# The branch hints of three engines read a second word of the flag

## The chip, the cores and the metric

The kernel runs on one core of a Trainium2 chip. The time is the device time of one execution in microseconds, given as the median of several runs. The core has five engines with instruction streams of their own: TensorE (PE; its weight loads are shown as PEld), VectorE (DVE), ScalarE (ACT), GpSimd (POOL) and SyncE (SP, which here issues most of the DMAs). An engine's sequencer also executes instructions that occupy no data path: register loads, branches, semaphore waits.

## What is computed

The reference works on x of 8 sequences x 128 tokens x 512 channels in float32 and adds two blocks to it. Cut to what matters:

```
x = x + ffn0(cond0(x))          # cond0: x @ W.T plus a gated low-rank term of two experts in eight
                                # ffn0: 4-bit weights (packed, with zeros and scales by groups), silu(gate) * up, down
x = x + ffn1(cond1(x))          # cond1: x[b] @ weight[id[b]].T, ffn1: rms norm, silu(gate) * up, down
```

In ffn0 a weight is `scale[g_idx[i]] * (q - (zero[g_idx[i]] + 1))`. The kernel has a fast way of handling scales that supposes the usual order of the group indices and scales of ordinary size, and a second, general way for any other input.

## The kernel before

The work is written out twice in one program. `network(..., True, ...)` is the whole computation with ffn0 done by groups of scales (`by_groups_of_scales`); behind it stands a branch, `tc.If(again[0] > 0, ...)` at L1719, and under it `network(..., False)`, the whole computation once more with ffn0 done in float32 (`in_float32`). With the inputs of this case the second one is never executed: each engine jumps over it to the end of the program.

What decides is a flag. `verdict` makes a count, for each of 128 partitions, of the conditions met by indices and scales. In the second block's plan the task "count" adds the counts by one small matmul (`met`, L971) into a PSUM bank, and the task "judge" (`told`, L974) compares the sum with the number wanted on VectorE and writes 1 into the flag if it is smaller, else 0. The flag is an int32 word in SBUF, with room around it (`FLAG_PLACE`).

The first block is in an order written by hand: ten and a last chunk of 128 inner channels, gate and up products on TensorE over four groups of the contraction and two halves of the tokens, with rescaling of the PSUM sums between groups by ScalarE or VectorE, which also unpack and dequantise the next chunks. The second block is ordered by a planner (`Plan`): every step is a task with an estimated time, its dependencies and a key (a due time), and the tasks are emitted in the order in which the planner's model begins them. The inner dimension has 14 chunks (`chunk`), each with 42 matmuls of 128x512 for gate and up; the weights are split into parts (`w`, `wz`), and the down products (`down`, L1628) run in blocks of two or three chunks. Each engine executes its own stream in that order.

The engines learn the flag in `high_low` (L1641): at the first product of the last down block every engine loads the word into a register (`values_load`), and TensorE, VectorE and ScalarE (the list `FETCHED`) get a branch hint named "again" that takes its value from this register. All of this stands in the engines' streams among matmuls and other work: TensorE's load comes between products of the last gate/up chunk (L1480) and down products (L1628). After the load SyncE also executes two check instructions of the sequencer. The branch itself (L1719) stands behind the last work of each engine, 20 us later. The outputs are written by SyncE, the last piece by ScalarE (L1690, L1692), and behind the branch SyncE waits for all output DMAs before the closing barrier (L1876).

Of the kernel before, what the change touches and what calls it, by code (L numbers as in the profile page):

```python
# [16 lines left out]
I32 = mybir.dt.int32  # L17
# [4 lines left out]
ALU = mybir.AluOpType  # L22

P = 128
# [76 lines left out]
GU_PLACE, FLAG_PLACE, COND_PLACE = 64, 24, 48  # L101
# [6 lines left out]
FETCHED = [EngineType.PE, EngineType.DVE, EngineType.Activation]  # L108
# [11 lines left out]
NGOOD = KC + NJ0 + 3 * (2 * NJ0 + KC)  # L120
# [12 lines left out]
class Plan:  # L133
# [5 lines left out]
    def add(self, name, engines, fn, deps=(), key=0.0, takes=(), gives=()):  # L139
        t = Task(name, engines, fn, deps, key, takes, gives)  # L140
        for d in t.deps:
            d.then.append(t)
        self.tasks.append(t)
        return t
# [77 lines left out]
def network_in(ctx, tc, a, out, by_groups, flag, again):  # L222
    nc = tc.nc
# [371 lines left out]
    def by_groups_of_scales():  # L595
# [375 lines left out]
            nc.tensor.matmul(ps[:1, :1], lhsT=count[0][:, 0:1], rhs=count[0][:, 1:2], start=True, stop=True)  # L971

        def told(ps):
            nc.vector.tensor_scalar(flag[:1], ps[:1, :1], float(NGOOD * P), None, ALU.is_lt)  # L974

        judges.append((met, told))


# [230 lines left out]
    def of(k, *who):  # L1209
        x = plan.place[k, who]  # L1210
        return late_tiles[x] if isinstance(x, tuple) else x

    def pe(us):
        return {"pe": us}
# [4 lines left out]
    def dve(n):  # L1219
        return {"dve": 0.075 + n / 960}  # L1220

    def either(n):
        return act(n) | dve(n)
# [177 lines left out]
    if judges:  # L1401
        judge = judges.pop()
        met = add(
            "count", pe(0.2), lambda _: judge[0](of("bank", "judge")), [normed[ROWS1[0]]], 2 * ROW, [("bank", ("judge",))]
        )
# [170 lines left out]
    def h_tile(j, tb):  # L1576
        x = of("h3", j, tb)
        return x if len(x.shape) == 3 else x.rearrange("p i n k -> p i (n k)")

    def down_weights(j, k):  # L1580
        raw = add(
            "wd", {"sp": 0.4}, lambda _: nc.sync.dma_start(out=of("wd", j), in_=a["wd1"][:, j, :]), [fd_open], k - 10.0,
            [("wd", (j,))],
        )

        def high(_):
            nc.scalar.activation(of("d", j)[:, 0], of("wd", j), AF.Copy, scale=HSCALE)

        def large(_):
            nc.scalar.activation(of("wd", j), of("wd", j), AF.Copy, scale=1.0 / EPS)  # L1590

        def low(_):
            d = of("d", j)
            nc.vector.scalar_tensor_tensor(d[:, 1], d[:, 0].bitcast(F32), -1.0 / EPS, of("wd", j), ALU.mult, ALU.add)

        def diff(_):
            d = of("d", j)
            nc.vector.tensor_tensor(d[:, 2], d[:, 0].bitcast(F32), d[:, 1].bitcast(F32), ALU.subtract)

        t0 = add("d hi", act(D), high, [raw], k, [("d", (j,))])  # L1600
        t1 = add("d large", act(D), large, [t0], k)
        t2 = add("d lo", dve(D), low, [t1], k, (), [("wd", (j,))])
        t3 = add("d di", dve(D), diff, [t2], k)
        d_ready[j] = (t0, t2, t3)

    def down(j0, j1):
        k, n = begin["down", j0], j1 - j0
        last = j1 == NJ1
        for j in range(j0, j1):
            down_weights(j, k - DOWN_LEAD + D_STEP * (j - j0))  # L1610
        users = []
        parts = [(tb, m, 0, TB) for tb in range(NTB) for m in range(KC)]
        if last:
            tb, m = parts.pop()[:2]
            parts += [(tb, m, c0, c0 + TB // 2) for c0 in (0, TB // 2)]
        for i, (tb, m, c0, c1) in enumerate(parts):
            kk = k + 3 * n * PASS * i
            who = ("down", j0, m, tb, c0)
            mine, t, w = [], None, c1 - c0
            one = PASS * w / TB + (0.007 if w < TB else 0.0)  # L1620

            d_first = last and i >= NTB * KC - 1
            first_key = k + 3 * n * PASS * (NTB * KC - 1) - D_FIRST
            firsts = (2, j0) if d_first else (0, j0)

            def products(j, which, m=m, tb=tb, who=who, c0=c0, c1=c1, firsts=firsts):
                for i in which:
                    nc.tensor.matmul(  # L1628
                        of("bank", *who)[:, : c1 - c0],
                        lhsT=of("d", j)[:, i, m * P : (m + 1) * P],  # L1630
                        rhs=h_tile(j, tb)[:, i, c0:c1],
                        start=((i, j) == firsts),
                        stop=True,
                        skip_group_check=(i, j) != firsts,
                    )

            def sums(t, key, takes=()):
                for j in range(j0, j1):
                    def high_low(_, j=j, products=products, tell=(last and i == 0 and j == j0)):
                        if tell and by_groups:  # L1640
                            again.append(nc.values_load(flag[:1, :], min_val=0, max_val=1))  # L1641
                            tc.mark_branch_hint_location("again", hint=again[0], engines=FETCHED)
                        products(j, (0, 1))

                    t = add(
                        "down H", pe(2 * one), high_low, [*h_ready[j, tb][:2], *d_ready[j][:2], t], key,
                        takes if j == j0 else (),
                    )
                    mine.append((j, t))
                return t  # L1650

            def differences(t, key, some, takes=()):
                def fn(_, products=products):
                    for j in some:
                        products(j, (2,))

                needs = [x[2] for j in some for x in (h_ready[j, tb], d_ready[j])]
                t = add("down D", pe(len(some) * one), fn, [t, *needs], key, takes)
                mine.extend((j, t) for j in some)
                return t  # L1660

            def rescaled(t, by, key):
                def fn(e, who=who, w=w):
                    ps = of("bank", *who)[:, :w]
                    scaled(e, ps, ps, by)

                return add("rescale", either(w), fn, [t], key)

            takes = [("bank", who)]
            if d_first:  # L1670
                t = None
                for j in range(j0, j1):
                    t = differences(t, first_key, [j], takes if j == j0 else ())
                t = rescaled(t, DSCALE, first_key)
                t = sums(t, kk)
            else:
                t = sums(None, kk, takes)
                t = rescaled(t, HLSCALE, kk + R_AT)
                t = differences(t, kk + (DD_LAST if last and i == NTB * KC - 2 else DD_AT), range(j0, j1))
            by_end = 1.0 + EPS if d_first else -EPS  # L1680

            def done(_, i=i, m=m, who=who, by_end=by_end, cols=slice(tb * TB + c0, tb * TB + c1)):
                x = xT[:, m, cols]
                ps = of("bank", *who)[:, : cols.stop - cols.start]
                nc.vector.scalar_tensor_tensor(x, ps, by_end, x, ALU.mult, ALU.add)  # L1685
                if last:
                    by = nc.scalar if i == NTB * KC - 1 else nc.sync
                    if i == 1:
                        some = out[: 2 * P, cols].rearrange("(m p) t -> p m t", p=P)
                        by.dma_start(out=some, in_=xT[:, :2, cols])  # L1690
                    elif i > 1:
                        by.dma_start(out=out[m * P : (m + 1) * P, cols], in_=x)  # L1692

            add("done", dve(w), done, [t], kk + DONE_AT, (), [("bank", who)])
            users += [(j, tb, t) for j, t in mine]
        for j in range(j0, j1):
            for tb in range(NTB):
                add("h3", {None: 0.0}, None, [t for jj, tt, t in users if (jj, tt) == (j, tb)], k, (), [("h3", (j, tb))])
            add("d", {None: 0.0}, None, [t for jj, _, t in users if jj == j], k, (), [("d", (j,))])
# [11 lines left out]
@with_exitstack  # L1711
def adaln_ffn_kernel(ctx: ExitStack, tc: tile.TileContext, a, out):
    nc = tc.nc

    outer = ctx.enter_context(tc.tile_pool(name="outer", bufs=1, side="right"))
    flag = outer.tile([P, FLAG_PLACE], I32, name="flag")[:, :1]
    again = []
    network(tc, a, out, True, flag, again)
    with tc.If(again[0] > 0, preferred_fallthrough_block=True, label="again", name="again"):  # L1719
        network(tc, a, out, False)  # L1720
# [160 lines left out]
```

## Time and profile before

| | us |
|---|---|
| median of 3 runs | 413.8 (413.66 to 414.06) |
| the profiled execution | 413.65 |
| its span, first to last instruction | 411.6 |
| busy: TensorE | 405.0 |
| busy: VectorE | 368.2 |
| busy: ScalarE | 304.4 |
| last matmul begins | 406.3 |
| last VectorE instruction ends | 407.1 |
| SyncE sees the last output landed | 409.9 |

The profile is of one execution. Times in it count from the start of the span. Of a group of instructions by line the three durations are shortest, median and longest in ns; an engine name with a q (PEldq, DVEq, SPq) is a sequencer's instruction, during which the data path may go on with what was issued before. The granted TensorE clock was 0.999 over the span. The trace also records DMA packets, among them the fetches of instructions, which come in pieces of 16 KB for TensorE and of 8 KB for other engines.

### The profile page before, as it was taken

How to read it: one execution, taken by the hardware profiler on the slowest of the kernel's cores; microseconds unless marked ns; L12 is line 12 of the kernel's file. 1: busy time of each engine (PE TensorE's matmuls, PEld its weight loads, DVE VectorE, ACT ScalarE, POOL GpSimd, SP SyncE). 2: the span in 40 equal slices, each digit the busy share in tenths (PEclk: the TensorE clock that was granted, in tenths of full speed). 3: DMA queues.
4: the chain of work that ended last, by engine and by line, in shares of the span. 5: the costliest groups of instructions: out<-in, count | busy, mean ns of one | idle time of the engine just before them, and what ended most of it. 6: DMA issues, size and time to landing. Idle time of an engine off the chain costs nothing.

```text
span 411.6 us, 5202 instructions
## 1 busy us (share of the span) xinstructions
PE 405.0 (98%) x1779; PEld 319.3 (78%) x1779; DVE 368.2 (89%) x677; ACT 304.4 (74%) x502; POOL 28.9 (7%) x35
## 2 busy tenths in 40 slices
PE   9999999999999999999999999999999999999995
PEld 9886788888888867445778888888888888888884
DVE  4998989997999788988999999989999899988974
ACT  5943788858896786487999888867976688767751
POOL 1000200000000400421020011011011101000000
PEclk9999999999999999999999999999999999999999
DMA  8930820120020540782153214313423225000005
GB/s 282 398 150 7 254 73 7 46 58 2 0 64 2 197 135 2 257 303 40 51 160 73 64 25 125 100 31 92 110 57 91 73 45 135 4 2 1 25 2 209
DMA packets 17041, 38.59 MB, mean 94 GB/s; under 512 B 1904, under 2 KB 8944, under 8 KB 15984
## 3 DMA queue, kind: packets, MB, share of 16 engines
q1 hardware_dynamic: 11472, 25.09, 18.7%
q0 software_dynamic: 5104, 12.72, 12.1%
q10 hardware_dynamic: 432, 0.39, 0.3%
q8 instruction: 15, 0.25, 0.2%
q14 instruction: 18, 0.15, 0.1%
HBM read 36.10 MB, written 2.10 MB: 93 GB/s over the span
## 4 chain that ended last, share of the span: by engine, by line
PE 91%; DVE 5%; ACT 2%; issue 0%; DVEq 0%
PE bank L1480 30%; PE bank L1628 19%; PE down L731 9%; PE gate L681 9%; PE up L681 9%; PE bank L1292 6%; PE base L532 5%; PE experts L435 2%; PE base L558 2%; PE idle L388 1%; DVE xt L1260 1%; DVE a L1257 1%; PE bank L1333 1%; DVE down L315 1%; ACT h L337 0%
## 5 line engine op out<-in xcount | busy, mean ns | idle before, releaser
L1227 ACT ACTIVATE bank<-bank 128x512 f32<-128x512 f32 (+1 forms) x126 | 71.2, 581 | 23.4 <-PE bank L1480 14.0
L1628 PE MATMUL bank<-h,d 128*128 128x512 f32 (+1 forms) x249 | 67.3, 382 | 0.0
L1628 PEld LDWEIGHTS bank<-h,d 128*128 128x128 f32 x249 | 45.6, 188 | 9.2 <-DVE h L1105 0.2
L681 PE MATMUL gate<-a,dq 128*128 128x512 f32 (+1 forms) x176 | 47.7, 393 | 0.0
L681 PE MATMUL up<-a,dq 128*128 128x512 f32 (+1 forms) x176 | 47.4, 391 | 0.0
L1480 PE MATMUL bank<-a,w 128*128 128x512 f32 x168 | 45.2, 391 | 0.4 <-ACT snap L1227 0.4
L1480 PE MATMUL bank<-xs,w 128*128 128x512 f32 x168 | 44.3, 390 | 0.0
L731 PE MATMUL down<-h,wd 128*128 128x512 f32 (+1 forms) x176 | 41.7, 391 | 0.1
L731 PEld LDWEIGHTS down<-h,wd 128*128 128x128 f32 (+1 forms) x176 | 32.9, 188 | 7.9 <-DVE h L700 0.5
L681 PEld LDWEIGHTS gate<-a,dq 128*128 128x128 f32 (+1 forms) x176 | 32.5, 185 | 8.2 <-ACT gate L313 0.6
L681 PEld LDWEIGHTS up<-a,dq 128*128 128x128 f32 (+1 forms) x176 | 32.4, 185 | 7.9 <-DVE a L824 0.3
L1480 PEld LDWEIGHTS bank<-a,w 128*128 128x128 f32 x168 | 31.2, 188 | 7.8 <-ACT snap L1227 0.8
L313 ACT ACTIVATE gate<-gate,ratio 128x1024 f32<-128x1024 f32 (+1 forms) x26 | 28.2, 1086 | 11.4 <-PE gate L681 11.3
L1480 PEld LDWEIGHTS bank<-xs,w 128*128 128x128 f32 x168 | 31.4, 188 | 6.5
L1227 ACT ACTIVATE snap<-bank 128x512 f32<-128x512 f32 x42 | 25.0, 596 | 13.6 <-PE bank L1480 13.3
L1108 DVE SCALAR_TENSOR_TENSOR w<-w 128x512 fp32r<-128x512 f32 x50 | 34.3, 687 | 0.1
L1685 DVE SCALAR_TENSOR_TENSOR xT<-bank,xT 128x512 f32<-128x512 f32 (+1 forms) x41 | 27.5, 676 | 4.2 <-PE bank L1628 3.8
L1095 POOL DMA_DIRECT2D raw<-in_wgu x14 | 17.2, 1228 | 197.1 <-PE up L681 44.8
L1514 DVE SCALAR_TENSOR_TENSOR snap<-bank,snap 128x512 f32<-128x512 f32 x42 | 28.4, 687 | 2.1 <-PE bank L1480 2.0
L1628 PE MATMUL bank<-w,d 128*128 128x512 f32 x96 | 30.0, 389 | 0.0
L1105 DVE TENSOR_TENSOR w<-raw,w 128x512 fp32r<-128x512 f32 x42 | 28.7, 686 | 0.2 <-ACT w L1102 0.2
L1292 PE MATMUL bank<-w,xT 128*128 128x512 f32 x64 | 28.9, 594 | 0.0
(169 smaller groups left out, 741.3 us busy)
## 6 DMA issues: line engine op xcount, KB each, us to landing
raw<-in_wgu SPq DMA_DIRECT2D x13, 640.0 KB, 3.9
raw<-in_wgu POOLq DMA_DIRECT2D x14, 256.0 KB, 4.5
wd<-in_wd SPq DMA_DIRECT2D x14, 256.0 KB, 2.7
qw<-in_qw_gu SPq DMA_DIRECT2D x5, 512.0 KB, 4.7
xT<-in_xT SPq DMA_DIRECT2D x2, 1024.0 KB, 11.9
xb<-in_first SPq DMA_DIRECT2D x7, 256.0 KB, 4.8
out<-xT SPq DMA_DIRECT2D x5, 256.0 KB, 2.1
qwd<-in_qw_d SPq DMA_DIRECT2D x2, 512.0 KB, 8.8
```

Source lines behind the costliest of these rows:

```text
L313: nc.scalar.activation(ps, ps, AF.Copy, scale=by)
L532: nc.tensor.matmul(base[m], lhsT=wT3[i][:, m, c * P : (c + 1) * P], rhs=x_parts(tb)[i][:, c, :], start=(i == 0 and c == 0), stop=(i == 1 a ...
L681: nc.tensor.matmul(ps, lhsT=dqs[j][:, c, half, :], rhs=a3[i][:, c, tb * TB : (tb + 1) * TB], start=(c == 0 and i == 0), stop=(i == 1), ski ...
L731: nc.tensor.matmul(ps[:, tb], lhsT=wds[k][:n, m * P : (m + 1) * P], rhs=h2[k][i][:, tb], start=(first and i == 0), stop=(i == 1), skip_gro ...
L1105: nc.vector.tensor_tensor(lo, raw, hi.bitcast(F32), ALU.subtract)
L1108: nc.vector.scalar_tensor_tensor(di, lo.bitcast(F32), -1.0 / EPS, hi.bitcast(F32), ALU.mult, ALU.add)
L1227: nc.scalar.activation(out_, in_, AF.Copy, scale=by)
L1292: nc.tensor.matmul(of("bank", "ad", b), lhsT=xT[:, c, b * T : (b + 1) * T], rhs=of("w1", b)[:, c * D : (c + 1) * D], start=(c == 0), stop= ...
L1480: nc.tensor.matmul(ps, lhsT=w[:, i, n, c * P : (c + 1) * P], rhs=x[i][:, c0 + c], start=(first and i == which[0] and c == 0), stop=True, s ...
L1514: nc.vector.scalar_tensor_tensor(x, of("bank", j, bank_), by, x, ALU.mult, ALU.add)
L1628: nc.tensor.matmul(of("bank", *who)[:, : c1 - c0], lhsT=of("d", j)[:, i, m * P : (m + 1) * P], rhs=h_tile(j, tb)[:, i, c0:c1], start=((i, ...
L1685: nc.vector.scalar_tensor_tensor(x, ps, by_end, x, ALU.mult, ALU.add)
```

## The change

`told` writes two words: the first as before (1 if the count is smaller than wanted), the second its opposite (1 if it is not smaller). The register that decides the branch is loaded from the first word as before, on all engines. TensorE, VectorE and ScalarE load the second word into another register, and their hints take their value from it. With this case's inputs the hint's value is 1 instead of 0.

```diff
         def told(ps):
-            nc.vector.tensor_scalar(flag[:1], ps[:1, :1], float(NGOOD * P), None, ALU.is_lt)
+            for i, op in enumerate((ALU.is_lt, ALU.is_ge)):
+                nc.vector.tensor_scalar(flag[:1, i : i + 1], ps[:1, :1], float(NGOOD * P), None, op)
...
                         if tell and by_groups:
-                            again.append(nc.values_load(flag[:1, :], min_val=0, max_val=1))
-                            tc.mark_branch_hint_location("again", hint=again[0], engines=FETCHED)
+                            again.append(nc.values_load(flag[:1, :1], min_val=0, max_val=1))
+                            met = nc.values_load(flag[:1, 1:], min_val=0, max_val=1, engines=FETCHED)
+                            tc.mark_branch_hint_location("again", hint=met, engines=FETCHED)
...
-    flag = outer.tile([P, FLAG_PLACE], I32, name="flag")[:, :1]
+    flag = outer.tile([P, FLAG_PLACE], I32, name="flag")[:, :2]
```

In the instruction streams this adds on VectorE one 1x1 comparison and one register load, on ScalarE one register load, and on TensorE one register load and, behind its hint, two sequencer instructions of the kind that SyncE has behind its load. The rest of the program that is executed keeps its order.

## The prediction

> **What bounds the kernel now.** I read the page first: the busy shares and the chain that ended last.
>
> ```profile
> span 411.6 us, 5202 instructions
> ...
> PE 405.0 (98%) x1779; PEld 319.3 (78%) x1779; DVE 368.2 (89%) x677; ACT 304.4 (74%) x502; POOL 28.9 (7%) x35
> ...
> PE 91%; DVE 5%; ACT 2%; issue 0%; DVEq 0%
> ```
>
> TensorE is busy for 98% of the span and is 91% of the chain: a pause of TensorE in the middle is paid at the end, unless TensorE would have waited later anyway. The edit touches three places: the judge (L974), the loads of the flag and the hints (L1641), and the branch at the end (L1719). So next I asked for these lines.
>
> ```profile
> L1641 SPq TENSOR_LOAD <-flag x1: 487/487/487, 173.5 to 173.5; - x1
> L1641 SPq FUSED_REGOPS  x1: 181/181/181, 174.1 to 174.1; - x1
> L1641 SPq SEQ_ASSERT  x1: 28/28/28, 174.3 to 174.3; - x1
> ...
> L1641 DVEq TENSOR_LOAD <-flag x1: 537/537/537, 383.8 to 383.8; - x1
> L1641 PEldq TENSOR_LOAD <-flag x1: 493/493/493, 384.0 to 384.0; - x1
> L1641 ACTq TENSOR_LOAD <-flag x1: 467/467/467, 384.2 to 384.2; - x1
> ```
>
> One load of a flag word into a register takes 0.47 to 0.54 us of an engine's sequencer. Only SyncE now has the two instructions that follow a load whose value is checked against its bounds (FUSED_REGOPS, SEQ_ASSERT). Does such a load hold up its engine? The timeline of TensorE's weight loads says:
>
> ```profile
> 383.78 0.41 PEld L1480 LDWEIGHTS bank<-xs,w 128*128 128x128 f32 x2
> 384.23 0.41 PEld L1480 LDWEIGHTS bank<-xt,w 128*128 128x128 f32 x2
> 384.73 0.37 PEld L1628 LDWEIGHTS bank<-w,d 128*128 128x128 f32 x2
> ```
>
> Pairs follow each other every 0.453 us (383.78, 384.23), so the third was due at 384.68 and came at 384.73. In the trace's nanoseconds TensorE's register load runs from 384.042 to 384.535, its hint from 384.642 to 384.686, and the late weight load starts 0.043 us after that. So the sequencer's lead over the array was used up to the last 0.05 us: whatever is added here stands in full in TensorE's time.
>
> Then the end, by the branch's line:
>
> ```profile
> L1719 PEldq COMPARE_BRANCH  x1: 402/402/402, 405.0 to 405.0; - x1
> L1719 PEldq EVENT_SEMAPHORE  x1: 51/51/51, 406.7 to 406.7; - x1
> L1719 DVEq COMPARE_BRANCH  x1: 84/84/84, 406.7 to 406.7; - x1
> L1719 ACTq COMPARE_BRANCH  x1: 68/68/68, 406.8 to 406.8; - x1
> L1719 SPq COMPARE_BRANCH  x1: 53/53/53, 407.5 to 407.5; - x1
> L1719 ACTq EVENT_SEMAPHORE  x1: 17/17/17, 410.0 to 410.0; - x1
> L1719 DVEq EVENT_SEMAPHORE  x1: 21/21/21, 410.2 to 410.2; - x1
> ```
>
> After its branch TensorE executes the next instruction at 406.66, right behind its last matmul. VectorE and ScalarE stand for 3.43 us (406.755 to 410.181) and 3.19 us (406.855 to 410.042), although what they wait for, their own last instruction, is done by 407.1. The trace's instruction fetches (8 KB for these two engines, 16 KB for TensorE) explain it: fetches start at 407.997 and 408.104, some 1.24 us after these two branches; between the hints at 384.4 to 384.7 and 407.9 no 8 KB fetch is recorded at all. TensorE has one at 398.849, in its usual step of about 29 us, and was not held up at its jump over more than a thousand rows. I read this so: with a hint of 0, the next fetch that falls due brings the jump's target; TensorE had one due before its branch, the other two had not. The end itself is none of these engines': SyncE sees its last output land at 409.90, then makes its list of waits until 410.65 and closes the barrier.
>
> **The change part by part.** *Order.* Only the added instructions differ. VectorE gets a second 1x1 comparison behind L974 and one register load at L1641; ScalarE gets one register load; TensorE gets one register load and the two check instructions behind the hint. SyncE and GpSimd get nothing, no DMA is added or moved, and no queue is passed.
>
> *Second comparison (VectorE, 173.4).* The first takes 140 ns, and the next VectorE instruction starts 69 ns after its start. In TensorE's waits between 168 and 200 us VectorE is named once, with 0.2 us. I take 0; the ends are 0 and 0.14 us (the new instruction wholly on the path, and the judge's PSUM bank free that much later).
>
> *Second register load on TensorE.* Nothing in the trace has two such loads in a row. Lower end: they overlap and only an issue step of about 0.05 us is added (the step from hint to weight load is 0.043). Upper end: a load of VectorE's length and TensorE's gap behind it, 0.537 + 0.107 = 0.64. I take the nearest row, TensorE's own load, one after the other: 0.493 + 0.107 (the gap from load to hint) = 0.600 us, because in every row of a load the engine's next instruction starts only after the load's end.
>
> *The two checks on TensorE.* From SyncE's rows: 0.050 + 0.181 + 0.050 + 0.028 = 0.309 us. Lower end 0.18 (the long one alone, the gaps hidden). Upper end: TensorE's semaphore waits take 0.051 where SyncE's take 0.017, three times as much; with the short one tripled, the gaps at 0.107 and the long one half as long again, 0.107 + 0.27 + 0.107 + 0.084 = 0.57. I take 0.31.
>
> So TensorE stands for 0.600 + 0.309 = **0.91 us** more: the weight load of 384.73 comes at 385.64. The ends are 0.05 + 0.18 = 0.23 and 0.64 + 0.57 = 1.21.
>
> [...]
>
> *Does it pass to the end?* From 385 to 406.6 the chain of waits is TensorE without a break. TensorE idles there once: a matmul at 396.70 is followed after 0.338 instead of 0.227 us, waiting for VectorE's h (L1105). That h goes back through ScalarE's sl (393.31) to a TensorE bank that ends at 393.3, so it moves along. Nothing is absorbed, and the last matmul, the last outputs and SyncE's waits all come 0.91 later.
>
> *Second loads on VectorE and ScalarE.* VectorE: 0.537 + 0.076 after a hint that ended at 384.43, so its next instruction is ready at about 385.05 instead of 384.94: 0.1 to 0.15 late. ScalarE: 0.467 + 0.063, so its snapshot of 385.11 comes at about 385.37. Both lie inside TensorE's own pause (until 385.64), which covers them; without that pause up to 0.26 us would show, if TensorE waited for that bank at once. Zero.
>
> *The hint's value.* If 1 means the opposite of 0, TensorE's fetch at 398.8 brings the code that follows in order, and TensorE then stands at its branch as the other two do. Priced from their rows: about 3.4 us, and a 16 KB fetch takes 1.13 us where theirs take 0.38 to 0.44, so some 4.1. From 405.08 + 0.91 it is back at 410.1. SyncE asks for TensorE's count at 410.585 + 0.91 = 411.5. So 1.4 us of cover are left, and the cost is 0. VectorE and ScalarE had no fetch due in the first place and stand as before, with 0.34 us to spare (410.18 against SyncE's question at 410.53), which moves along. If the cover were gone, each microsecond more would be paid.
>
> [...]
>
> *Sum.* The profiled execution took 413.65 us: the span of 411.6 and 2.05 around it; it is 0.15 below the median of 413.8. 413.65 + 0.91 = 414.56, or by the median 413.8 + 0.91 = **414.7 us**.
>
> **The rivals.** The bound of measurement, about 0.2%, is 0.83 us here.
>
> (1) *The loads overlap.* For it: independent loads need not wait for each other. Against: each row shows the engine's sequencer still until the load ends. TensorE's pause is then 0.05 + 0.31 = 0.36 us, the time 414.2: no difference.
>
> (2) *TensorE's missed jump shows at the end.* For it: TensorE's fetch is the longest. If a second fetch is needed before it can go on (1.2 us to start, 1.13 to arrive), it is back at 410.1 + 2.3 = 412.4, past 411.5, and 0.9 are added: 415.6. It decides from 1.4 us of extra stall. Against: TensorE has 1.4 us in hand.
>
> (3) *The value means the reverse, so that the change brings VectorE's and ScalarE's targets early* (the not-slower side). Their stalls of 3.4 and 3.2 us go, but SyncE's last landing stays. What could move is that landing: the last SyncE output takes 2.8 us from issue where the median of the out transfers is 2.1, with four instruction fetches in the same stretch. All of it gone is 0.7 us: 413.8 + 0.91 - 0.7 = 414.0, no difference; with the overlap of rival 1, 413.8 + 0.36 - 0.7 = 413.5. It ends faster than the bound only if TensorE's pause is near zero and the landing gains more than 0.83. Against it: TensorE's jump was free with a hint of 0.
>
> **How the numbers follow.** The serial pause has 0.69; it lies a little above the bound at 0.91, and its own ends run from 0.78 (0.60 + 0.18) to 1.21, so I count 0.50 of it as slower and 0.19 as no difference. Rival 1 has 0.14, nearly all no difference (0.12; 0.02 faster by a lucky end). Rival 2 has 0.10, slower. Rival 3 has 0.07: 0.04 faster, 0.03 no difference. Together: slower 0.60, same 0.34, faster 0.06. The range runs from 414.0 (the lower end of the pause, 0.23) to 415.6 (rival 2).
>
> **What would show it.** Right: two register loads in a row at TensorE near 384, the second starting after the first's end; FUSED_REGOPS and SEQ_ASSERT behind the hint; the weight load of 384.73 at about 385.6; and the last matmul at about 407.3. TensorE's semaphore wait behind its branch at about 410 instead of 406.7, and SyncE's last landing still the end. Wrong: loads that overlap; a barrier that waits for TensorE; 8 KB fetches right behind the hints and no stall of VectorE and ScalarE; or a pause that a later wait of TensorE swallows.

## The result, and the profile after

The changed kernel takes 414.50 us (median of 22 runs, 413.99 to 415.13), the kernel before, run beside it, 413.99 (413.52 to 414.67). The ratio is 1.0014, 95% interval 1.0008 to 1.0020: slower by 0.58 us (0.33 to 0.83). That is clear of zero, and by the bound of 0.2% which the prediction set it counts as "no difference".

The profiled execution of the changed kernel has a span of 412.6 us. Its page begins so:

```profile
span 412.6 us, 5208 instructions
...
PE 405.7 (98%) x1779; PEld 319.6 (77%) x1779; DVE 368.2 (89%) x678; ACT 304.4 (74%) x502; POOL 29.1 (7%) x35
...
PE 91%; DVE 5%; ACT 2%; issue 1%; DVEq 0%
```

Six instructions more, as many matmuls as before, and 1% of the chain in which TensorE waited for nothing that the profile shows ("issue"), where there was 0%. The timeline of TensorE's weight loads shows where (start, length in us; in brackets the idle time ahead):

```profile
384.07 0.41 PEld L1481 LDWEIGHTS bank<-xs,w 128*128 128x128 f32 x2
384.53 0.41 PEld L1481 LDWEIGHTS bank<-xt,w 128*128 128x128 f32 x2
385.75 0.30 PEld L1629 LDWEIGHTS bank<-w,d 128*128 128x128 f32 x2 [0.81 <-issue]
386.09 0.66 PEld L1481 LDWEIGHTS bank<-a,wz 128*128 128x128 f32 x3
```

The weight load that was 0.05 us late is now 0.77 us late: due at 384.98, it comes at 385.75. What stands there is on two lines of the source, the old load (L1642; first the shortest, median and longest time in ns, then the start)

```profile
L1642 DVEq TENSOR_LOAD <-flag x1: 536/536/536, 384.1 to 384.1; - x1
L1642 PEldq TENSOR_LOAD <-flag x1: 489/489/489, 384.3 to 384.3; - x1
L1642 ACTq TENSOR_LOAD <-flag x1: 467/467/467, 384.5 to 384.5; - x1
```

and the new one (L1643):

```profile
L1643 DVEq TENSOR_LOAD <-flag x1: 322/322/322, 384.7 to 384.7; - x1
L1643 PEldq TENSOR_LOAD <-flag x1: 309/309/309, 384.9 to 384.9; - x1
L1643 ACTq TENSOR_LOAD <-flag x1: 292/292/292, 385.0 to 385.0; - x1
L1643 PEldq FUSED_REGOPS  x1: 167/167/167, 385.5 to 385.5; - x1
L1643 PEldq SEQ_ASSERT  x1: 28/28/28, 385.7 to 385.7; - x1
```

The loads do not overlap: TensorE's second starts at 384.934, 0.106 us after the first's end. But it takes 0.309 us, not 0.489, and on VectorE and ScalarE the second load is shorter than the first in the same way (0.322 for 0.536, 0.292 for 0.467).

At the end, by the branch's line:

```profile
L1721 SPq EVENT_SEMAPHORE  x8: 17/17/17, 409.0 to 410.9; - x8
...
L1721 PEldq COMPARE_BRANCH  x1: 4157/4157/4157, 406.0 to 406.0; - x1
...
L1721 PEldq EVENT_SEMAPHORE  x1: 51/51/51, 410.2 to 410.2; - x1
L1721 ACTq EVENT_SEMAPHORE  x1: 17/17/17, 411.0 to 411.0; - x1
L1721 DVEq EVENT_SEMAPHORE  x1: 21/21/21, 411.2 to 411.2; - x1
```

TensorE's branch took 0.40 us before and takes 4.16 now; it is back at 410.2 (forecast: 410.1), while SyncE sees its last output at 410.94 and closes the barrier after that. (The output that is issued last is one of SyncE's, at 407.1 in the kernel before; ScalarE's piece goes out ahead of it, at 406.4.) VectorE and ScalarE stand as long as before, 3.43 and 3.20 us.

To see what passes to the end I compare the starts of equal matmuls in the two traces, one by one. The changed kernel's are 0.27 us later from the first input on (the matmuls of L532 begin at 12.43 instead of 12.16 us; the offset is another in another execution, 0.66 us in the run with early hints below), still 0.30 later at the last matmul ahead of the loads, and 1.00 later some fifteen matmuls behind them, where the difference stays to the last one. So the pause is a step of 0.71 us, and nothing of it is recovered. In what follows "the step" is this number.

### The profile page after: what moved, and what is told of

It is laid out like the page before. It is cut to its first block, busy times and chain, and to the rows that moved or that the text cites. A ratio compares the mean times of both kernels' runs of the same rounds, so it can differ in the third digit from the quotient of the medians.

```text
span 412.6 us, 5208 instructions
## 1 busy us (share of the span) xinstructions
PE 405.7 (98%) x1779; PEld 319.6 (77%) x1779; DVE 368.2 (89%) x678; ACT 304.4 (74%) x502; POOL 29.1 (7%) x35
## 4 chain that ended last, share of the span: by engine, by line
PE 91%; DVE 5%; ACT 2%; issue 1%; DVEq 0%
PE bank L1481 30%; PE bank L1629 19%; PE down L731 9%; PE gate L681 9%; PE up L681 9%; PE bank L1293 6%; PE base L532 5%; PE experts L435 2%; PE base L558 2%; PE idle L388 1%; DVE xt L1261 1%; DVE a L1258 1%; PE bank L1334 1%; DVE down L315 1%; ACT h L337 0%
```

## The experiments

Theory A, from the prediction: the time is lost in TensorE's pause, made of the second load and its two checks; the hint's value costs nothing, because TensorE's missed jump is hidden under the landing of the outputs. Rival B: the value costs the time, at the end. Rival C: the second comparison or the loads on VectorE and ScalarE do.

**The value back to 0, all instructions kept** (of the changed kernel)

```diff
-            for i, op in enumerate((ALU.is_lt, ALU.is_ge)):
+            for i, op in enumerate((ALU.is_lt, ALU.is_lt)):
```

> The changed kernel with both words written by the same comparison, so that the hint's value is 0 again; every instruction stays. Theory A (the cost is TensorE's pause at the second load and its two checks, the value costs nothing): TensorE's matmuls fall behind by the same 0.73 us at 385, the time is that of the changed kernel, 1.0014 of before within 0.0007; only TensorE's branch changes, from 4.16 us back to 0.40. Rival B (the value 1 costs the time, through TensorE's missed jump at the end): the time is that of before.

Measured: 1.0022 of before (1.0013 to 1.0031), a step of 0.73 us, TensorE's branch 0.41 us. The time did not come back with the jump. B falls. The ratio lies above the changed kernel's and a hair above what was expected (at most 1.0021), but the intervals overlap and the step is nearly the same (0.73 and 0.71 us).

**The value 1 with one load** (of the kernel before)

```diff
-            nc.vector.tensor_scalar(flag[:1], ps[:1, :1], float(NGOOD * P), None, ALU.is_lt)
+            nc.vector.tensor_scalar(flag[:1], ps[:1, :1], float(NGOOD * P), None, ALU.is_ge)
...
-    with tc.If(again[0] > 0, ...
+    with tc.If(again[0] < 1, ...
```

> One word, with the opposite meaning (1 if the conditions are met), the branch tests for smaller than 1, the hint takes this word: the value 1 without the second comparison, second load and checks. Theory A: no pause at 385, the time of before within 0.0007 of it, and TensorE's branch still takes 4.1 us, hidden under the outputs' landing. Rival B: 0.5 us slower than before, as the changed kernel.

Measured: 0.9996 (0.9987 to 1.0005), step 0.05 us. The branch's line:

```profile
L1719 PEldq COMPARE_BRANCH  x1: 4132/4132/4132, 405.4 to 405.4; - x1
...
L1719 PEldq EVENT_SEMAPHORE  x1: 51/51/51, 409.6 to 409.6; - x1
L1719 ACTq EVENT_SEMAPHORE  x1: 17/17/17, 410.4 to 410.4; - x1
L1719 DVEq EVENT_SEMAPHORE  x1: 21/21/21, 410.6 to 410.6; - x1
```

So the two halves of the change are apart: the value makes the jump 3.7 us longer and costs no time that can be measured; the instructions that fetch it cost what the change costs.

**No checks** (of the changed kernel)

```diff
-                            met = nc.values_load(flag[:1, 1:], min_val=0, max_val=1, engines=FETCHED)
+                            met = nc.values_load(flag[:1, 1:], min_val=0, max_val=1, engines=FETCHED,
+                                                 skip_runtime_bounds_check_because="a comparison gives 0 or 1")
```

> The changed kernel without the bounds check of the second load: TensorE loses FUSED_REGOPS and SEQ_ASSERT. Theory A: the pause falls by the 0.31 us from the end of the hint's step to the weight load, from 0.73 to 0.4; the time is 0.2 us above before, 1.0005 to 1.001. Rival: the checks are hidden under the restart of the array, and the pause stays at 0.7.

Measured: 1.0005 (0.9996 to 1.0014), step 0.37 us. The weight loads of this kernel:

```profile
384.46 0.41 PEld L1481 LDWEIGHTS bank<-xt,w 128*128 128x128 f32 x2
385.37 0.30 PEld L1629 LDWEIGHTS bank<-w,d 128*128 128x128 f32 x2 [0.49 <-issue]
```

The two checks are 0.34 us of the 0.71, the second load is the other 0.37. It is the step that tells this kernel from the changed one; the intervals of their times overlap. Only TensorE pays for the checks: they stand on it alone.

**The second comparison alone** (of the changed kernel)

```diff
-                            met = nc.values_load(flag[:1, 1:], min_val=0, max_val=1, engines=FETCHED)
-                            tc.mark_branch_hint_location("again", hint=met, engines=FETCHED)
+                            tc.mark_branch_hint_location("again", hint=again[0], engines=FETCHED)
```

> Only the second comparison of the change: VectorE writes both words, but the hints take the first word's register and nothing else is loaded. Theory A: no difference from before (within 0.0007), no step of the matmuls at 173 or at 385. Rival C (VectorE's comparison or the longer hold of the judge's bank costs): up to 0.14 us, and a step of that size after 173 us in the matmuls' starts against before.

Measured: 1.0004 (0.9995 to 1.0013), and no step at 385 (0.001 us). Around 173 us the matmuls' difference against before changes by less than 0.05 us. Of C, the comparison is out.

**A third load on TensorE** (of the changed kernel)

```diff
-                            met = nc.values_load(flag[:1, 1:], min_val=0, max_val=1, engines=FETCHED)
+                            nc.values_load(flag[:1, 1:], min_val=0, max_val=1, engines=[EngineType.PE])
+                            met = nc.values_load(flag[:1, 1:], min_val=0, max_val=1, engines=FETCHED,
+                                                 skip_runtime_bounds_check_because="a comparison gives 0 or 1")
```

> The changed kernel with one more load of the second word on TensorE alone: load, load, the two checks, a third load, hint. Theory A: each further load stops TensorE for its own length and gap; if a load is short (0.31 instead of 0.49 us) because it comes soon after another, the third one adds 0.309 + 0.107 = 0.41 us, pause 1.14 us; if it is short only directly behind another, 0.6 and 1.33 us. Time 0.9 to 1.2 us above before (1.0022 to 1.003). Rival (loads hide behind each other and the pause is a restart of the array): 0.73 as in the changed kernel.

Measured: 1.0026 (1.0016 to 1.0036), step 1.08 us, 0.37 more than with two loads. The third load:

```profile
L1644 PEldq TENSOR_LOAD <-flag x1: 303/303/303, 385.4 to 385.4; - x1
```

With the checks between it and the second it is short as well. So a further load on TensorE costs about what it lasts and its gap (0.40 us from its start to the hint's), and "directly behind another" is not what makes it short.

**Second load and hint apart** (of the changed kernel)

```diff
-    def high_low(_, ..., tell=(last and i == 0 and j == j0)):
+    def high_low(_, ..., tell=(last and i == 0 and j == j0), then=(last and i == 1 and j == j0)):
         if tell and by_groups:
             again.append(nc.values_load(flag[:1, :1], min_val=0, max_val=1))
-            met = nc.values_load(flag[:1, 1:], min_val=0, max_val=1, engines=FETCHED)
+        if then and by_groups:
+            met = nc.values_load(flag[:1, 1:], min_val=0, max_val=1, engines=FETCHED,
+                                 skip_runtime_bounds_check_because="a comparison gives 0 or 1")
             tc.mark_branch_hint_location("again", hint=met, engines=FETCHED)
```

> The second load and the hint stand ten matmuls later, ahead of the first product of the next down bank, without checks. Theory A: a load costs only what goes beyond the sequencer's lead over the array. Alone, the first load without its hint is covered; the second one has its full length again (0.49 with 0.11 and the hint's 0.05) but a lead of its own of some 0.5 us, so that 0.0 to 0.2 us are left in all and the time is that of before within 0.0007. Rival (a load stops the array for its length wherever it stands): 0.6 us behind before.

Measured: 0.9992 (0.9983 to 1.0001), step 0.001 us. The weight loads run on without a gap:

```profile
384.09 0.41 PEld L1481 LDWEIGHTS bank<-xt,w 128*128 128x128 f32 x2
384.54 0.41 PEld L1629 LDWEIGHTS bank<-w,d 128*128 128x128 f32 x2
385.00 0.87 PEld L1481 LDWEIGHTS bank<-a,wz 128*128 128x128 f32 x4
385.90 0.41 PEld L1481 LDWEIGHTS bank<-xt,w 128*128 128x128 f32 x2
```

The second load of TensorE in this kernel:

```profile
L1644 PEldq TENSOR_LOAD <-flag x1: 313/313/313, 385.7 to 385.7; - x1
```

The same load, also without checks, that costs 0.37 us behind the first costs nothing eight matmuls later, because the sequencer has its lead over the array again, 0.70 us: the load begins at 385.653 while the weight load that follows the hint is not due before 386.356. My expectation of its length was wrong: 1.26 us after the first one's end it still took 0.313 us and not 0.49. This kernel has the change's value in its hints, two words and two loads on each of the three engines (but not the two checks), and none of its cost. So of Rival C the second loads on VectorE and ScalarE are out as well: both are there, and TensorE has no pause that could hide them. The kernel does not beat the kernel before in a way that the interval shows.

**No hints** (of the kernel before)

```diff
                             again.append(nc.values_load(flag[:1, :], min_val=0, max_val=1))
-                            tc.mark_branch_hint_location("again", hint=again[0], engines=FETCHED)
```

> The kernel before without any hint. Theory A: the hint instruction is TensorE's 0.05 us at 385, so the matmuls come 0.0 to 0.05 us earlier; TensorE misses its jump at the end as with the value 1 (branch 4.1 us), hidden; the time of before within 0.0007. Rival (no hint is not the same as the value 1, which switches the fetch of the target off): branch 0.4 us.

Measured: 0.9996 (0.9987 to 1.0005), TensorE's branch 4.25 us, no gap at 385. Without a hint the jump is as long as with the value 1 (4.25 and 4.13 us), so 1 behaves here as "no hint"; 0 leaves a jump of 0.40 us. The hints of the kernel before bring nothing that can be measured.

**The hints three chunks earlier** (of the kernel before)

```diff
-    def high_low(_, ..., tell=(last and i == 0 and j == j0)):
+    def high_low(_, ..., tell=(j0 == 8 and i == 0 and j == j0)):
```

> The kernel before with load and hints (value 0) three chunks earlier, in the down block that begins near 340 us, so that VectorE and ScalarE too have an instruction fetch due between hint and branch. If the hint makes the next due fetch bring the target in place of the code that follows: no stall of VectorE and ScalarE behind the branch (410.2 and 410.0 become 407), but TensorE and the others miss the code that follows one block later and stall there by 3 to 4 us: 417 to 418. If the target is fetched only from the block that holds the branch: TensorE as before, VectorE and ScalarE are served only if their fetch at 361 to 374 is due in that block, and the time is that of before, since SyncE's wait for the outputs ends the span.

Measured: 0.9999 (0.9989 to 1.0008). The branch's line:

```profile
L1719 PEldq EVENT_SEMAPHORE  x1: 51/51/51, 407.3 to 407.3; - x1
...
L1719 ACTq EVENT_SEMAPHORE  x1: 17/17/17, 407.9 to 407.9; - x1
L1719 DVEq EVENT_SEMAPHORE  x1: 21/21/21, 407.9 to 407.9; - x1
```

Behind their branches VectorE goes on after 0.5 us instead of 3.4 and ScalarE after 0.4 instead of 3.2, and the time does not move. No engine stalled in the middle (from 335 us to the end the instructions of TensorE, VectorE and ScalarE stay 0.66 to 0.67 us behind those of the kernel before), so the early hint held none of them up ahead of the branch. The 8 KB fetches of this run lie at 361.7 and 362.5 where the kernel before has them at 361.3 and 374.0; why the second one moved by 12 us I did not find out. In this run the two lie between the hints (near 340) and the branches and the stalls are short; in the kernel before none does (hints at 384.4 to 384.7, next 8 KB fetch at 407.997) and the stalls are long. Which code a fetch brings, no run shows.

**Sixteen matmuls behind TensorE's last work**, with the value 0 and 1 (of the kernel before, and of the one with the value 1 and one load)

```diff
     plan.run()
+    if by_groups:
+        for _ in range(16):
+            nc.tensor.matmul(bank_tiles[7], lhsT=xs[0][:, 0, :P], rhs=xs[0][:, 1], start=True, stop=True)
     order_stack.close()
```

> The kernel before with 16 more matmuls of 128x512 behind TensorE's last work (their result is used by nothing), hint value 0. They take 16 x 0.227 = 3.6 us and end near 410.2, before the barrier at 410.8. Theory A: the jump costs 0.4 us of sequencer time under the matmuls, and the time is that of before plus 0.0 to 0.3 us.

> The same 16 matmuls behind TensorE's last work, one word with the opposite meaning and hint value 1. The cover over TensorE's missed jump, 1.4 us in the changed kernel, is gone. Theory A: TensorE's branch begins near 409 and takes 4.1 us, so TensorE is back near 413 and closes the barrier 2 to 2.5 us later than before: 416 to 416.5. Rival (the missed jump costs nothing even without cover): as with the value 0.

Measured: 1.0012 (1.0002 to 1.0022) for both; branches of 0.40 and 4.33 us. The expectation failed for a plain reason: I let the branch begin near 409, but it began at 406.20 and 406.63, 0.22 us ahead of the first of the sixteen matmuls in both, since the sequencer had issued all of them ahead of it. The stall ran under the matmuls, and the pair doesn't test the end. (With the value 0 the ratio is also above what I expected, at most 0.3 us more; the interval reaches down to that.) Hence the next pair.

**One matmul that waits for VectorE's last instruction**, with the value 0 and 1

```diff
     plan.run()
+    if by_groups:
+        nc.tensor.matmul(bank_tiles[7][:, :256], lhsT=ident, rhs=xT[:, KC - 1, NT - 256 :], start=True, stop=True)
     order_stack.close()
```

> The kernel before with one more matmul on TensorE (its result is used by nothing) that reads the last piece of the output and so waits for VectorE's last instruction: TensorE's branch cannot be issued before about 407.1. Hint value 0. Theory A: the branch takes 0.4 us, TensorE is done near 407.7, SyncE's outputs end the span as before; the time of before within 0.0007.

> The same late branch, with the word of opposite meaning and hint value 1. Theory A: the branch begins near 407.15 and takes 4.1 to 4.3 us, so TensorE's count comes at 411.4, where SyncE asks for it at 410.6: SyncE waits for TensorE, and the span ends 0.7 to 0.9 us later than with the value 0, 1.0015 to 1.0025 of before. Rival (the missed jump costs nothing at the end, however late): no difference between the two.

Measured: 1.0004 (0.9993 to 1.0015) with 0, and 1.0023 (1.0014 to 1.0032) with 1. The branch's line with the value 0:

```profile
L1721 PEldq COMPARE_BRANCH  x1: 397/397/397, 407.3 to 407.3; - x1
...
L1721 PEldq EVENT_SEMAPHORE  x1: 51/51/51, 408.0 to 408.0; - x1
```

and with the value 1:

```profile
L1721 SPq EVENT_SEMAPHORE  x8: 17/17/17, 408.3 to 411.2; - x8
...
L1721 PEldq COMPARE_BRANCH  x1: 4089/4089/4089, 407.5 to 407.5; - x1
...
L1721 PEldq EVENT_SEMAPHORE  x1: 51/51/51, 411.6 to 411.6; - x1
```

So with a late branch the value 1 does cost time, although the two intervals overlap by a hair; the size, 0.8 us by the ratios, was forecast. The way was not, in the one traced execution: SyncE asked for TensorE's count at 411.89, when it had been there since 411.66. What SyncE waited for was its own last output, seen at 411.21 (with the value 0: at 410.06). Fifteen of the sixteen parts of this output had landed by 410.01 and the last one at 411.19, in a stretch with a 16 KB instruction fetch of 1.30 us from 408.72 and an 8 KB one of 0.99 us from 408.88. With a punctual landing TensorE at 411.66 would have been the last instead. Fetches in that stretch did not by themselves make the landing late: the run with the value 0 has them too (16 KB from 408.61, 8 KB from 408.71, but shorter, 0.99 and 0.65 us), and its last part landed at 410.04. The single times bear on how often the one or the other decides. With the value 0, nine of twelve lie at 413.4 to 414.3 us and three at 415.1 to 415.5, so a late end comes without the long jump too. With the value 1, four of eleven lie at 414.3 to 414.6 and seven at 415.0 to 415.4, the traced one among them. No run tells the two ways apart.

## Why the prediction was right or wrong, point by point

The time (414.5 in a range of 414.0 to 415.6) and the direction hold. The loss was mis-sized: 0.91 us forecast, 0.58 (0.33 to 0.83) measured, and the chance of 0.60 for "slower by over 0.2%" was too much against the 0.34 for "no difference", which is what came. That 414.7 lies only 0.2 us off is partly luck: the loss was added to 413.8, and the kernel before took 413.99 beside the changed one.

- *The bound and the way to the end*: right. The step of 0.71 us passes undiminished to the last matmul. SyncE's last output is seen 1.04 us later than in the kernel before, where the last matmul is 1.00 later.
- *Second register load on TensorE, 0.600 us*: this is the mis-sized term. From the second load's start to the hint's it is 0.410 us (0.309 + 0.101). I took TensorE's own row, and the row was of a first load; every later load of this flag in the runs is shorter (0.29 to 0.32 us against 0.47 to 0.54). That loads do not overlap was right.
- *The two checks, 0.309 us*: right. From the hint's start to the weight load 0.410 us, before 0.087, so 0.32; taken out, they gave back 0.34.
- *Second comparison, 0; loads on VectorE and ScalarE, 0*: right for the comparison by itself. The loads made less delay than the 0.1 to 0.26 us forecast: with the offset of 0.30 us taken off, VectorE's next instruction comes 0.00 and ScalarE's snapshot 0.09 us late, inside TensorE's pause. Without that pause, in the kernel with load and hint apart, nothing showed either.
- *The hint's value, 0 and 1.4 us of cover*: right. That the next fetch due brings the jump's target was my reading of the times; what a fetch brings, no run shows. The runs show TensorE's branch at 0.40 to 0.41 us with the value 0, and at 4.1 to 4.3 us with the value 1 or without a hint. TensorE came back at 410.23, and SyncE asked for its count at 411.62. That the forecast 410.1 is so close is partly luck: it started from a branch at 405.08, where the row before has 405.00, and this execution's offset of 0.30 us more than makes up for the 0.20 by which the step fell short.
- *Rival 1, the loads overlap*: no. Its loss of 0.36 us even lies nearer to the measured 0.58 than my 0.91, but by chance: the second load is short, it does not overlap. *Rival 2, the jump shows at the end*: not here. TensorE needed no second fetch before it went on: it was back at 410.23, and its next 16 KB fetch began at 410.88. The jump does show once the branch begins 1.4 us later (407.45 against 406.00), though in the traced execution by way of the outputs' landing. *Rival 3, the value means the reverse*: no; with 0 TensorE's branch takes 0.40 us, with 1 it takes 4.1 to 4.3 us, as in the kernel without hints (4.25).

## What to carry to other kernels

In these runs a sequencer's instruction on the engine that bounds the kernel was free while the sequencer was far enough ahead of the data path (the second load begun 0.70 us ahead of the weight load behind it: a step of 0.001 us), and cost about its length and gap where the lead was used up (a load of 0.31 us and a gap of 0.10: a step of 0.37 us). So look how late the next instruction comes, and put two such instructions some matmuls apart rather than behind each other. The bounds check of a loaded value stood on one engine alone, SyncE at the first load and TensorE, the busy one, at the second, and cost TensorE about as much as the load (0.34 and 0.37 us). What the branch hint was worth lay behind the branch: all three jumps could be 0.4 to 0.5 us or 3.0 to 4.3 us long, and the time stayed the same (0.9996 to 0.9999 of before) as long as the outputs were still on their way.

## What the runs showed of the hardware that I had not expected

- Loads of the flag after the first one on an engine take 0.29 to 0.32 us instead of 0.47 to 0.54, also with two checks between (0.303) or 1.26 us later (0.313). Whether it is the place in memory or the recent use, no run tells apart.
- The output that ends the span has stragglers. In the kernel before, the last output's sixteen parts land at 408.80 in the median, and the last three at 409.78 to 409.88; with VectorE's, ScalarE's and SyncE's instruction fetches in that stretch (from 408.00, 408.10 and 408.63). Whether the fetches delay the output by some of this microsecond is not shown: no run took them away, since the engines fetch after their jumps with an early hint too (at 408.56, 408.61 and 409.22).
- TensorE's sequencer issued sixteen independent matmuls, 3.6 us of work, ahead of a branch (branch at 406.20, first of the sixteen at 406.42). At the flag the lead was much less: the first load begins 0.64 us before the weight load behind it is due.
